# Experts' stage of a metaformer kernel: gating two blocks behind, pooled sums with the probabilities standing, choice on the logits, another order of the pools

## The chip, the cores and the metric

The kernel runs on one core of a Trainium2 chip. The metric is the device time of one execution in microseconds (us). Five engines take part, each with its own queue of instructions that it works off in order: PE (TensorE, matrix products and transposes; PEld are its loads of the standing operand), DVE (VectorE), ACT (ScalarE), POOL (GpSimd) and SP (SyncE), which here issues the DMAs.

## The reference, cut to what matters

The model is two metaformer layers on x of shape (4, 128, 64, 64): convolution with neighbourhood attention, a recurrence over the sequence, eight mamba layers, and a layer of experts that choose tokens. The change concerns the last of these. There are B = 4 sequences of S = 4096 tokens with D = 128 features, E = 64 experts with hidden size H = 512, and every expert takes the K = 8 tokens of a sequence with the highest probability.

```python
x = _ln_t(tokens)
logits = jnp.einsum('bsd,ed->bse', x, gate_w) + gate_b
probs = jax.nn.softmax(logits, axis=1)                 # over the tokens
vals, idx = jax.lax.top_k(probs.transpose(0, 2, 1), K)
...
pooled = jnp.einsum('bked,bke->bed', gathered, topv)    # sum of the 8 tokens by probability
h = gelu(einsum('ebd,edh->ebh', h, weight1))            # with a bias row
out = einsum('ebh,eho->ebo', h, weight2)                # with a bias row
...
outputs.at[arange(Bn)[:, None], flat_idx].add(weighted) # out by probability, back to the 8 tokens
```

The kernel does not gather. It makes a map of probabilities over all 4096 tokens that is zero except at an expert's eight tokens, and takes both sums as matrix products with that map.

## The kernel before

One program runs four stages one after the other: the conv layer, the recurrence, mamba and `experts`. The first three share a set of memory pools, which are released before the experts open theirs; a tile that is placed where an earlier one lay waits for the last use of the earlier one. The body stands under `tc.manual_schedule()`, so the order of the instructions on each engine's queue is the order in which the program writes them, and no scheduler moves any. In the experts' stage the order is therefore the one of the loop at L1386.

The four sequences are worked on as two pairs. A pair has 4096 tokens per sequence, in NBLK = 8 blocks of 512, so the loop runs n = 0 to 15 over blocks, and once more to finish. The feature dimension lies on the 128 partitions in the input, and the tiles are these:

- `fetch(n)` (L1233) loads block n of both sequences. It runs three blocks ahead.
- L1244 to L1259 load the gate's weights and the vector of biases, and make `both`: 128 columns that take the mean out of a token, and 64 columns of the gate's weights with the mean taken out.
- `tokens(n)` (L1269) does, for each of the two sequences, four products L1279 into `pa` (128 tokens by 192), copies the 128 token columns to a token slab (ACT, L1285) and the 64 gate columns to `raw` (ACT, L1286), squares the tokens (POOL, L1290) and sums the squares (DVE, L1291). Two small ACT instructions make 1/sigma of each token, `r` (L1293, L1294).
- `gating(n)` (L1296) multiplies `raw` by `r` (POOL, L1301), transposes it four times (PE, L1304), so that 2 x 64 (sequence, expert) rows lie on the partitions and tokens along the row, adds the bias into the logits `lg` (DVE, L1308) and takes the block's eight highest per row (DVE, L1309). In the loop it follows one block behind `tokens`: in iteration n, `tokens(n)` comes first and `gating(n - 1)` after it.
- `softmax(pr)` (L1313) takes the eight highest of the row, subtracts the highest in an exponential over all 4096 (ACT, L1321) that also sums, and makes the eight best probabilities. `scaled` (L1328) divides by the sum. `others` (L1333) writes `rest`, the row with its eight best replaced by zero.
- `pick(pr, i)` (L1340) subtracts `rest` from the row in block i (DVE, L1345), so that only the chosen ones remain, transposes the block back (PE, L1349), multiplies by `r` out of PSUM into `pk` (DVE, L1352), and adds the pooled sums up with eight products, one for each 128 tokens of each sequence: the 128 tokens x 128 features stand in the array and the 64 probabilities of a sequence move (PE, L1363, 16 records in the profile). `pooled` (L1368) copies the sums to `pz`.
- A ring of seven slabs of 2 MB holds the tokens (two slabs per pair) and the experts' weights. `give(s)` (L1377) issues the four DMAs of weight slab s. Slabs 0 to 2 are given during the loop, 3 and 4 take the place of pair 0's tokens, and the others follow when their slab is free.

Pair 0's softmax falls into iteration 9, its scaling and `others` into iteration 10, its picks two each into iterations 12 to 15. Pair 1's follow after the loop. Then come the experts' products L1429 (first weights) and L1464 (second weights, both with 32 standing columns in four column groups of one PSUM tile), and the output from L1485 on: the products of the map with the experts' outputs (L1498), the addition to x (L1505) and the stores.

## Time and profile before

| | us |
|---|---|
| median of 3 runs | 15860.6 (15850.09 to 15864.64) |
| the profiled execution's own time | 15855.17 |
| its span | 15853.2 |
| span of the experts' stage, from about 15510 on | some 343 |
| of it: picks of pair 1 | 15705.8 to 15748.2 |
| of it: weights, experts' products, output | 15748.2 to 15853.2 |

Times in the profile are microseconds from the start of the span. The groups of PE in the experts' stage are given as line, engine, operation, names (out<-in), shapes, count | busy us, mean ns of one | idle time of the engine before them, and what ended it:

```profile
L1279 PE MATMUL pa<-both,x 128*128 128x192 f32 x256 | 60.9, 408 | 1.1 <-DMA x<-x_d 1.1
L1363 PE MATMUL pp<-pk,slab 128*128 128x64 f32 x256 | 58.8, 424 | 12.5 <-DVE pk L1352 12.5
L1464 PE MATMUL po<-slab,hz 128*32 128x128 f32 x512 | 27.4, 342 | 12.3 <-DMA slab<-in_w_dram 11.4 <-DVE hz L1445 0.8
L1349 PE MATMUL pt<-ident,lg 128*128 128x128 f32 x64 | 17.1, 423 | 23.0 <-DVE lg L1345 23.0
L1304 PE MATMUL pg<-ident,raw 128*128 128x128 f32 x64 | 13.9, 356 | 47.1 <-POOL raw L1301 47.1
```

Records of PE overlap, so the mean of one is longer than the distance from one to the next. PE waited 47.1 us for the raw products of POOL, 23.0 us for DVE's subtractions and 12.5 us for DVE's `pk`.

### The profile page before, as it was taken

To read this page: it belongs to the slowest core of one execution; us is meant where nothing else is said; L and a number is where in the kernel's file an instruction comes from. 1 tells how busy PE (TensorE), PEld (TensorE's weight loads), DVE (VectorE), ACT (ScalarE), POOL (GpSimd) and SP (SyncE) were. 2 spreads that over 40 slices of the span, in tenths; PEclk is the share of its full clock that TensorE was granted. 3 is DMA by queue.
4 is the path that set the end of the run, shared out by engine and by line. 5 is a ranking of instruction groups with operands and counts; after the bars stand their busy time and mean duration, and the time that the engine had idled before them with its cause. 6 is when DMAs were issued, how large, how long until landed. Compare 5 with 4: busy or idle time off the path is not lost. (4 is left out here: it accounts for less than half of the span.)

```text
span 15853.2 us, 302528 instructions
## 1 busy us (share of the span) xinstructions
PE 14462.2 (91%) x120338; PEld 10877.7 (69%) x120338; DVE 13680.6 (86%) x14939; ACT 12003.3 (76%) x23543; POOL 13174.3 (83%) x9086
## 2 busy tenths in 40 slices
PE   7888779999999999999999999999999999989996
PEld 3444567777777777777777777777777777666665
DVE  8998049998999889998999899989998999899993
ACT  6887258887788778877888788878887788777771
POOL 4554049998999999998999899989998999899992
PEclk8999579999999999999999999999999999999997
DMA  0000012222222222222222222222222222222224
GB/s 21 22 25 19 15 57 103 98 97 104 97 103 103 95 102 98 99 107 95 103 99 98 100 98 103 103 99 101 99 98 102 99 103 100 96 99 94 101 102 153
DMA packets 423331, 1431.56 MB, mean 90 GB/s; under 512 B 204064, under 2 KB 204448, under 8 KB 290720
## 3 DMA queue, kind: packets, MB, share of 16 engines
q1 hardware_dynamic: 421920, 1412.21, 24.3%
q8 instruction: 951, 15.58, 0.4%
q14 instruction: 460, 3.77, 0.1%
HBM read 1353.34 MB, written 58.72 MB: 89 GB/s over the span
## 5 line engine op out<-in xcount | busy, mean ns | idle before, releaser
L1028 DVE TENSOR_TENSOR_SCAN hs<-dA,state,dBx 128x512 f32<-128x512 f32 x7168 | 8703.2, 1263 | 1048.9 <-PE dBx L995 1010.3
L1044 POOL TENSOR_TENSOR hs<-hs,Cb 128x2048 f32<-128x2048 f32 x2048 | 9294.1, 4538 | 165.8 <-POOL state L1041 1.3
L973 ACT ACTIVATE dA<-dt,A 128x512 f32<-128x512 f32 x7168 | 4734.5, 721 | 7.4 <-DVE hs L1028 1.2
L1048 PE MATMUL yT<-ident,hs 128*128 128x128 f32 x32768 | 4351.9, 277 | 7.5 <-POOL hs L1044 7.5
L1048 PEld LDWEIGHTS yT<-ident,hs 128*128 128x128 f32 x32768 | 3797.0, 144 | 771.3 <-issue 644.1
L995 PE MATMUL dBx<-diag,dtxT 64*128 64x128 f32 x57344 | 4191.7, 286 | 122.9 <-DVE hs L1028 110.5
L995 PEld LDWEIGHTS dBx<-diag,dtxT 64*128 64x128 f32 x57344 | 3518.0, 188 | 1087.3 <-issue 712.1
L672 ACT ACTIVATE z<-p 128x4 f32<-128x4 f32 x4096 | 710.2, 173 | 1855.2 <-PE p L669 1849.1
L669 PE MATMUL p<-z,vt 128*128 128x4 f32 x8192 | 1578.7, 263 | 205.2 <-ACT z L672 203.4
L669 PEld LDWEIGHTS p<-z,vt 128*128 128x128 f32 x8192 | 1350.5, 207 | 587.2 <-ACT z L672 303.2
L1016 POOL TENSOR_TENSOR hs<-Bb,dtx 128x512 f32<-128x512 f32 x1024 | 1274.0, 1277 | 0.3 <-PE yT L1048 0.3
L1028 DVE TENSOR_TENSOR_SCAN hs<-dAp,state,hs 128x512 f32<-128x512 f32 x1024 | 1228.5, 1262 | 0.0
L961 DVE TENSOR_TENSOR diag<-f,i 128x512 f32<-128x512 f32 x1792 | 1158.9, 671 | 8.3 <-PE f L949 8.3
L860 DVE SCALAR_TENSOR_TENSOR xc<-f,taps,xc 128x509 f32<-128x509 f32 (+2 forms) x1536 | 1131.3, 737 | 37.6 <-ACT tail L855 10.4
L1041 POOL COPY state<-hs 128x4 f32<-128x4 f32 x2048 | 386.7, 189 | 845.4 <-DVE hs L1028 844.9
L1126 ACT ACT_TABLE_LOAD x771 | 989.2, 1283 | 10.5
L278 DVE SCALAR_TENSOR_TENSOR acc<-qp,dww,acc 128x512 f32<-128x512 f32 x1184 | 888.7, 751 | 12.2
L973 ACT ACTIVATE dAp<-dt,A 128x512 f32<-128x512 f32 x1024 | 708.8, 692 | 212.7 <-DVE hs L1028 180.5
L875 PE MATMUL f<-u,given 128*128 128x512 f32 x1024 | 510.6, 621 | 331.1 <-ACT pos L1094 323.2
L849 ACT ACTIVATE xc<-f,taps 128x509 f32<-128x509 f32 x512 | 350.4, 684 | 478.1 <-PE f L846 476.0
L934 POOL TENSOR_TENSOR dtx<-dt,xc 128x512 f32<-128x512 f32 x512 | 650.5, 1271 | 12.4 <-ACT dt L928 12.4
L944 ACT COPY dtxT<-f 128x512 f32<-128x512 f32 x512 | 298.2, 582 | 445.2 <-PE f L941 445.2
(231 smaller groups left out, 16232.3 us busy)
## 6 DMA issues: line engine op xcount, KB each, us to landing
Cb<-c_d SPq DMA_DIRECT2D x1024, 1024.0 KB, 4.6
Bb<-c_d SPq DMA_DIRECT2D x256, 512.0 KB, 5.5
given<-in_m_given_dram SPq DMA_DIRECT2D x64, 640.0 KB, 5.8
slab<-in_w_dram SPq DMA_DIRECT2D x64, 512.0 KB, 10.2
x<-x_d SPq DMA_DIRECT2D x96, 256.0 KB, 3.9
x_d<-x SPq DMA_DIRECT2D x64, 256.0 KB, 2.0
c_d<-dbl SPq DMA_DIRECT2D x512, 32.0 KB, 1.6
xb<-in_x_dram SPq DMA_DIRECT2D x32, 256.0 KB, 3.0
```

What stands on the lines that cost most here:

```text
L278: nc.vector.scalar_tensor_tensor(rows(to), x, dww[:, t : t + 1], rows(o.acc), ALU.mult, ALU.add)
L669: nc.tensor.matmul(self.p[:, k, :], self.vt, self.before, start=False, stop=True, skip_group_check=True)
L672: nc.scalar.activation(self.z[:, k, :], self.p[:, k, :], AF.Tanh, scale=0.5)
L860: nc.vector.scalar_tensor_tensor(x, o.v[h][:, : TL - k], taps[:, o.l, h, DC - 1 - k : DC - k], x, ALU.mult, ALU.add)
L961: nc.vector.tensor_tensor(o.diag[:, sp], bt.unsqueeze(2).to_broadcast([P, NB, 64, 2]), i64.unsqueeze(1).unsqueeze(3).to_broadcast([P, NB, ...
L973: nc.scalar.activation(o.dA[j][:, k, :], o.dt[h], AF.Exp, scale=A[:, o.l, h, n : n + 1])
L995: nc.tensor.matmul(o.dBx[j][:, at : at + 64, :], o.dtxT[h][row, n, :], o.diag[row, sp, n], start=True, stop=True,)
L1016: nc.gpsimd.tensor_tensor(hs[:, k, :].rearrange("p (q n t) -> p q n t", n=NB, q=2), o.Bb[:, k, :].rearrange("p (q n t) -> p q n t", n=NB, ...
L1028: nc.vector.tensor_tensor_scan(hs[:, k, :], o.dA[j][:, k, :], hs[:, k, :] if sp == SP_B else o.dBx[j][:, :, k], state[:, o.l, o.b, h, s : ...
L1044: nc.gpsimd.tensor_tensor(hs, hs, o.Cb[f], ALU.mult)
L1048: nc.tensor.matmul(o.yT[:, n, :], x[:, n * P : (n + 1) * P], ops.ident, start=start and n == 0, stop=True, is_transpose=True, skip_group_c ...
L1126: return lambda o: nc.scalar.preload_act_table_set(name)
```

## The change

1. The pools of mamba are opened in another order. The sizes stay the same, but what lies where changes, and with it what of a later stage lies over it.
2. The gate's weights are loaded and prepared at the start of the kernel, in `gating_weights`, and kept in a pool that stays open. The small tiles it needs meanwhile are released again before the conv layer opens its pools.
3. `gating` follows two blocks behind `tokens` (LAG = 2), with a third buffer for `raw`; the loop runs to n = 17.
4. The choice is made on the logits: `others` replaces the eight highest logits by -1e30, and only then comes the exponential over 4096, in place. The picks take the exponential of `rest` block by block (a new ACT instruction in `pick`) and subtract. The division by the sum is no longer made over the row; `pooled` and the copy of `oh` multiply by the reciprocal instead.
5. `pick` is cut in two. `add_picked(pr, i)` follows one block behind. In it `pk` stands in the array, 32 columns at a time, in four column groups of one PSUM tile (2 sequences x 2 halves of the experts), and the 128 features of the tokens move: 16 products per block, of which the profile shows two records each. The sums come out transposed, and `pooled` transposes them back.
6. Pair 0's picks stand in iterations 11 to 14. Its pooled sums and the DMAs of weight slabs 3 and 4 stand in iteration 15.
7. The bias b1 is loaded as two tiles behind the picks of pair 1 in the program, in buffers that held blocks of x.

```diff
-        c = ctx.enter_context(tc.tile_pool(name="mc", bufs=1))
-        wp = ctx.enter_context(tc.tile_pool(name="mwp", bufs=2))
-        w1 = ctx.enter_context(tc.tile_pool(name="mw1", bufs=1))
-        w = ctx.enter_context(tc.tile_pool(name="mwk", bufs=2))
-        w3 = ctx.enter_context(tc.tile_pool(name="mwk3", bufs=3))
         dap = ctx.enter_context(tc.tile_pool(name="mda", bufs=4))
         hsp = ctx.enter_context(tc.tile_pool(name="mhs", bufs=4))
         cbp = ctx.enter_context(tc.tile_pool(name="mcb", bufs=4))
+        w3 = ctx.enter_context(tc.tile_pool(name="mwk3", bufs=3))
+        w = ctx.enter_context(tc.tile_pool(name="mwk", bufs=2))
+        c = ctx.enter_context(tc.tile_pool(name="mc", bufs=1))
+        wp = ctx.enter_context(tc.tile_pool(name="mwp", bufs=2))
         up = ctx.enter_context(tc.tile_pool(name="mu", bufs=5))
+        w1 = ctx.enter_context(tc.tile_pool(name="mw1", bufs=1))
...
-def experts(tc, ops, I, x3_d, out):
+def gating_weights(tc, const, ops, I):
+    nc = tc.nc
+    both = const.tile([P, P + E], F32, name="both")
+    gateb = const.tile([P, 1], F32, name="gateb")
+    nc.sync.dma_start(out=gateb, in_=I["vec"][:, V_GATEB : V_GATEB + 1])
+    nc.vector.tensor_tensor(both[:, 0:P], ops.ident, ops.avg, ALU.subtract)
+    with tc.tile_pool(name="gw", bufs=1) as w, tc.tile_pool(name="gp", bufs=1, space=PSUM) as ps:
+        gate = w.tile([P, E], F32, name="gate")
+        nc.sync.dma_start(out=gate, in_=I["gate"])
+        p = ps.tile([P, E], F32, name="p")
+        nc.tensor.matmul(p, both[:, 0:P], gate, start=True, stop=True)
+        nc.vector.tensor_copy(both[:, P:], p)
+    return both, gateb
+def experts(tc, ops, I, gating_w, x3_d, out):
...
         nc.scalar.preload_act_table_set(EXP_LN)
-        gate = c.tile([P, E], F32, name="gate")
-        nc.sync.dma_start(out=gate, in_=I["gate"])
-        vec = c.tile([P, V_N], F32, name="vec")
-        nc.sync.dma_start(out=vec, in_=I["vec"])
+        both, gateb = gating_w
         for n in range(3):
             fetch(n)
-        b1 = c.tile([P, NQ, HID], F32, name="b1")
-        nc.sync.dma_start(out=b1, in_=I["b1"])
         b2 = c.tile([P, E], F32, name="b2")
         nc.sync.dma_start(out=b2, in_=I["b2"])
-        both = c.tile([P, P + E], F32, name="both")
-        nc.vector.tensor_tensor(both[:, 0:P], ops.ident, ops.avg, ALU.subtract)
-        pq = psb.tile([P, BLK], F32, tag="pg", name="pq")
-        nc.tensor.matmul(pq[:, 0:E], both[:, 0:P], gate, start=True, stop=True)
-        nc.vector.tensor_copy(both[:, P:], pq[:, 0:E])
...
         def tokens(n):
-            raw = raws[n] = w.tile([P, 4, 2, E], F32, tag="raw", name="raw")
+            raw = raws[n] = w.tile([P, 4, 2, E], F32, tag="raw", name="raw", bufs=3)
...
                     pg[:, m * P : (m + 1) * P], raw[:, m].rearrange("p k e -> p (k e)"), ops.ident
                 )
             lg = lgs[pr][:, i * BLK : (i + 1) * BLK]
-            nc.vector.tensor_scalar(lg, pg, vec[:, V_GATEB : V_GATEB + 1], None, ALU.add)
+            nc.vector.tensor_scalar(lg, pg, gateb, None, ALU.add)
             nc.vector.max(out=tops[pr][:, i, :], in_=lg)
-        rests, bests, tots = {}, {}, {}
-        def softmax(pr):
+        rests, negs, tots = {}, {}, {}
+        def others(pr):
             lg = lgs[pr]
             top = w.tile([P, 8], F32, tag="top", name="top")
             nc.vector.max(out=top, in_=tops[pr].rearrange("p n t -> p (n t)"))
-            neg = w.tile([P, 1], F32, tag="neg", name="neg")
+            neg = negs[pr] = w.tile([P, 1], F32, tag="neg", name="neg")
             nc.vector.tensor_scalar(neg, top[:, 0:1], -1.0, None, ALU.mult)
+            rest = c.tile([P, NG * NHC, NJ * 36], F32, tag="rp", name="rest")
+            rests[pr] = rest.rearrange("p a b -> p (a b)")[:, 0:L]
+            nc.vector.match_replace(
+                out=rests[pr], in_to_replace=top, in_values=lg, imm_value=-1e30
+            )
             tot = tots[pr] = w.tile([P, 1], F32, tag="tot", name="tot")
             nc.scalar.activation(lg, lg, AF.Exp, bias=neg, accum_out=tot)
-            best = bests[pr] = w.tile([P, 8], F32, tag="best", name="best")
-            nc.scalar.activation(best, top, AF.Exp, bias=neg)
             nc.vector.reciprocal(tot, tot)
-            nc.vector.tensor_scalar(best, best, tot, None, ALU.mult)
-        def scaled(pr):
-            nc.vector.tensor_scalar(lgs[pr], lgs[pr], tots[pr], None, ALU.mult)
-        def others(pr):
-            rest = rests[pr] = c.tile([P, NG * NHC, NJ * 36], F32, tag="rp", name="rest")
-            nc.vector.match_replace(
-                out=rest.rearrange("p a b -> p (a b)")[:, 0:L],
-                in_to_replace=bests[pr], in_values=lgs[pr], imm_value=0.0,
-            )
-        pps = {}
+        pts, pps = {}, {}
         def pick(pr, i):
             here = slice(i * BLK, (i + 1) * BLK)
-            lg = lgs[pr][:, here]
-            rest = rests[pr].rearrange("p a b -> p (a b)")[:, here]
+            lg, rest = lgs[pr][:, here], rests[pr][:, here]
+            nc.scalar.activation(rest, rest, AF.Exp, bias=negs[pr])
             nc.vector.tensor_tensor(lg, lg, rest, ALU.subtract)
-            pt = psb.tile([P, BLK], F32, tag="pg", name="pt")
+            pts[i] = psb.tile([P, BLK], F32, tag="pg", name="pt")
             for m in range(4):
                 o = (4 * i + m) * P
-                nc.tensor.transpose(pt[:, m * P : (m + 1) * P], lgs[pr][:, o : o + P], ops.ident)
+                nc.tensor.transpose(
+                    pts[i][:, m * P : (m + 1) * P], lgs[pr][:, o : o + P], ops.ident
+                )
+        def add_picked(pr, i):
             pk = w.tile([P, 4, 2, E], F32, tag="pk", name="pk")
             r = rs[pr][:, 4 * i : 4 * i + 4, :]
             nc.vector.tensor_tensor(
                 pk,
-                pt.rearrange("p (m k e) -> p m k e", m=4, k=2),
+                pts.pop(i).rearrange("p (m k e) -> p m k e", m=4, k=2),
                 r.unsqueeze(3).to_broadcast([P, 4, 2, E]),
                 ALU.mult,
             )
             if i == 0:
-                pps[pr] = [psc.tile([P, E], F32, tag=f"pp{k}", name="pp") for k in range(2)]
+                pps[pr] = psc.tile([P, P], F32, tag="pp", name="pp")
             for m in range(4):
                 n = 4 * i + m
-                for k in range(2):
+                for g in range(4):
+                    k, half = divmod(g, 2)
                     nc.tensor.matmul(
-                        pps[pr][k], toks[pr][k][:, n, :], pk[:, m, k, :],
-                        start=n == 0, stop=n == NT - 1,
+                        pps[pr][32 * g : 32 * g + 32, :],
+                        pk[:, m, k, 32 * half : 32 * half + 32],
+                        toks[pr][k][:, n, :],
+                        start=n == 0, stop=n == NT - 1, skip_group_check=True,
                     )
         def pooled(pr):
+            ps = w.tile([P, P], F32, tag="os", name="ps")
+            nc.vector.tensor_scalar(ps, pps[pr], tots[pr], None, ALU.mult)
+            pt = psb.tile([P, BLK], F32, tag="pg", name="pt")
+            nc.tensor.transpose(pt[:, 0:P], ps, ops.ident)
             to = pz.rearrange("p m (j t) -> p m j t", t=36)
             for k in range(2):
                 nc.vector.tensor_copy(
-                    to[:, :, :, 2 * pr + k], pps[pr][k].rearrange("p (m j) -> p m j", j=NJ)
+                    to[:, :, :, 2 * pr + k],
+                    pt[:, k * E : (k + 1) * E].rearrange("p (m j) -> p m j", j=NJ),
                 )
         weights = {}
...
                 here = slice(n * (L // 4), (n + 1) * (L // 4))
                 nc.sync.dma_start(out=t[:, here], in_=I[which][s % 8][:, here])
+        LAG = 2
         give(0)
-        for n in range(2 * NBLK + 1):
+        for n in range(2 * NBLK + LAG):
             if n < 2 * NBLK:
                 tokens(n)
                 if n + 3 < 2 * NBLK:
                     fetch(n + 3)
-            if n == 4:
-                give(1)
-            if n == 7:
-                give(2)
-            if n > 0:
-                gating(n - 1)
-            if n == NBLK + 1:
-                softmax(0)
-            if n == NBLK + 2:
-                scaled(0)
+            if n in (4, 7):
+                give(1 + n // 7)
+            if n >= LAG:
+                gating(n - LAG)
+            m = n - NBLK - LAG
+            if m == -1:
                 others(0)
-            if n >= 2 * NBLK - 4:
-                for i in range(2):
-                    pick(0, 2 * (n - 2 * NBLK + 4) + i) if n < 2 * NBLK else None
-            if n == 2 * NBLK - 1:
+            elif 1 <= m <= 4:
+                for i in range(2 * m - 2, 2 * m):
+                    pick(0, i)
+                    if i > 0:
+                        add_picked(0, i - 1)
+            elif m == 5:
+                add_picked(0, NBLK - 1)
                 pooled(0)
-        give(3)
-        give(4)
-        softmax(1)
-        scaled(1)
+                give(3)
+                give(4)
         others(1)
-        for i in range(NBLK):
-            pick(1, i)
+        for i in range(NBLK + 1):
+            if i < NBLK:
+                pick(1, i)
+            if i > 0:
+                add_picked(1, i - 1)
         pooled(1)
         hz = c.tile([P, NG * NHC, NJ * 36], F32, tag="rp", name="hz")
         nc.gpsimd.memset(hz, 0.0)
         hids, x3b = {}, {}
+        b1 = [w.tile([P, HID], F32, tag=f"x3{q}", name="b1", bufs=3) for q in range(NQ)]
+        for q in range(NQ):
+            nc.sync.dma_start(out=b1[q], in_=I["b1"][q])
         for q in range(NQ):
             ph = psb.tile([P, HID], F32, tag="pg", name="ph")
             for s in range(4 * q, 4 * q + 4):
...
                             start=j == 0, stop=j == NJ - 1, skip_group_check=True,
                         )
             hid = hids[q] = w.tile([P, HID], F32, tag="sq", name="hid")
-            nc.vector.tensor_tensor(hid, ph, b1[:, q, :], ALU.add)
+            nc.vector.tensor_tensor(hid, ph, b1[q], ALU.add)
             nc.scalar.activation(hid, hid, AF.Gelu)
         ohT = c.tile([P, B, E], F32, name="ohT")
         for q in range(NQ):
...
                 pt[:, 0:P], ohT[:, 2 * pr : 2 * pr + 2, :].rearrange("p b e -> p (b e)"), ops.ident
             )
             oh = w.tile([P, P], F32, tag="oh", name="oh")
-            nc.vector.tensor_copy(oh, pt[:, 0:P])
+            nc.vector.tensor_scalar(oh, pt[:, 0:P], tots[pr], None, ALU.mult)
             for i in range(NBLK // 2):
                 pa = [psa.tile([P, 2, BLK], F32, tag="pa", name="pa") for k in range(2)]
                 for m in range(2):
...
     nc.scalar.preload_act_table_set(EXP_LN)
     ops = Ops(nc, const)
+    gating_w = gating_weights(tc, const, ops, I)
...
             conv_layer(tc, ops, I, x1_d, wx_d, stats)
             rec = Recurrence(c, tc, ops, I, stats, wx_d, x1_d, x2_d)
             mamba(tc, ops, I, rec, x2_d, x3_d)
-        experts(tc, ops, I, x3_d, out)
+        experts(tc, ops, I, gating_w, x3_d, out)
...
-    o["b1"] = np.repeat(w1[:, P].reshape(2, P // B, HID), B, axis=1).transpose(1, 0, 2)
+    o["b1"] = np.repeat(w1[:, P].reshape(2, P // B, HID), B, axis=1)
```

## The prediction

> **What bounds it.** The page first.
>
> ```profile
> span 15853.2 us, 302528 instructions
> PE   7888779999999999999999999999999999989996
> PEclk8999579999999999999999999999999999999997
> ```
>
> The experts run in the last of 40 slices of 396 us (from about 15510). Outside it the change touches the kernel's first microseconds and the opening order of the mamba pools, so every gain comes from some 340 us. The stage table cuts them (columns: busy us and records of PE, PEld, DVE, ACT, POOL; granted clock; DMA share; GB/s):
>
> ```profile
> 15618.00:15690.60 72.60, 50.41 (x220) 45.73 (x221) 18.78 (x30) 6.70 (x18) 10.27 (x10) 0.64 0.00 0
> 15690.60:15705.80 15.20, 1.24 (x6) 0.84 (x6) 10.20 (x12) 3.99 (x3) 0.00 (x0) 0.50 0.73 276
> 15705.80:15748.20 42.40, 36.10 (x160) 32.92 (x160) 9.74 (x16) 0.00 (x0) 3.94 (x1) 0.50 0.00 0
> 15748.20:15810.60 62.40, 48.33 (x651) 24.75 (x650) 4.21 (x14) 2.54 (x3) 0.00 (x0) 0.83 1.01 396
> 15810.60:15853.20 42.60, 31.06 (x67) 10.05 (x67) 20.17 (x20) 0.00 (x0) 0.00 (x0) 0.74 0.89 358
> ```
>
> Picks of pair 0 among the last tokens (PE), a softmax in which PE stands still, picks of pair 1 (PE), and a tail of 105 us that the weight and output DMAs fill. The tail begins when pair 1's last product frees its token slabs, so what comes before it moves the end one for one. The chain of waits shows one pick (start, us):
>
> ```profile
> 15705.83 1.10 PE pt L1349 x4
> 15706.93 0.02 issue
> 15706.95 0.70 DVE pk L1352
> 15707.65 0.04 issue
> 15707.70 3.67 PE pp L1363 x16
> 15711.37 0.87 PE pt L1349 x4
> ```
>
> Transposes, DVE, product, next transposes: strictly one after the other, 5.31 us each.
>
> **The new product's price.** No row of before has it. Nearest is L1464, which also has 128x32 standing operands, 128 moving columns and four column groups (timeline):
>
> ```profile
> 15785.64 1.93 PE L1464 MATMUL po<-slab,hz 128*32 128x128 f32 x32 [0.87 <-DMA slab<-in_w_dram]
> 15792.22 4.72 PE L1464 MATMUL po<-slab,hz 128*32 128x128 f32 x96 [0.38 <-DVE hz L1445]
> ```
>
> Its single records come in fours that start within 0.02 us, 0.213 us from four to four at half clock and 0.109 at full. A product becomes 32 records, 8 fours: 1.71 us cold, 0.87 warm, against 3.67. Bounds: 0.9 (warm), 3.7 (no gain), 6.8 (32 x 0.213, if the groups ran in turn). I take 1.8 cold (1.71 and 0.1 for the drain below), because L1464 has the operand shapes and the same accumulator shared by four groups. [...] The trace has such a place in the conv layer, L432 (110*32, last at 1626.62) to L440 (128*128, 1626.93): 0.31 us where the pitch was 0.11, so 0.2. [...] I take 0.1 a product (1.6 in all) and keep 5 more for the range.
>
> **The clock.** The second place. [...] But L1363 holds the array 0.213 us for 64 moving columns. The column-tiled products of L1429, from 15748.93 on, brought full clock after 2.5 us (0.72 as the mean of 15748.2 to 15754.0: 2.5 us of 5.8 at full). Around L1464, bursts of 32 every 2.56 us with pauses, the clock switched to and fro. The new picks (1.7 of product, 0.87 of transposes) are nearest to that row: I take half of pair 1's picks at full clock; all cold or all warm goes to the range. [...]
>
> **Part by part** (program order is issue order on each engine).
>
> *Gating weights at the start.* Two DMAs go ahead of conv's on SP, and conv's first load (L156, issued at 0.73) waits in the new layout for the gate's landing and the small matmul that reads it. Gate issued at 1.18 (where L158 stands), landing after 1.7 (as L1244's did), matmul 0.6: about 3.75. All later conv loads stand behind it and the first matmul waits for x (10.97, "5.90 <-DMA xb"). **+3.0** (2.5 to 4).
>
> *Experts' start.* L1244 stood at 15516.71 behind x_d's write, L1246 and the fetch at 15517.57 behind it. Now the fetch waits for none of these and follows the issue at 15514.64: about 15515.1. Landing (2.8) and first matmul (15520.41) follow: **-2.3**. The DVE/PE work of L1257 to L1259 was hidden in that landing.
>
> *Two blocks behind.* POOL's order remains square, square, raw product, so block n-2's raw product still stands behind block n's squares, and PE's transposes and next tokens behind it (raw L1301 1.04, then L1304 idles "2.79 <-POOL raw L1301"). The period (6.05/7.55) stays; only the beginning has a stall fewer: third transposes at 15536.65 for 15540.32, **-3.6**. The third raw buffer costs nothing.
>
> *Choice on logits, pair 0.* Out go the scaling (L1328, 2.33) and best; the match (4.41 plus 0.09) comes ahead of the big exponential (3.71 plus 0.19), which overwrites its input and must wait. From T, the iteration's transposes: T 0.66, lg 0.75, maximum 0.69, top, negation, hand-overs: 2.5; match to 7.05; exponential to 10.9. Behind it on ACT stands the next token copy; POOL and PE wait for it, 3.73 later the next T: 14.6 for 10.16, **+4.4**. Next iteration 6.8 for 8.93 (no DVE scaling before the variances): **-2.1**. Picks now sit in iterations 11 to 14: 11 has two sets of transposes and one product between T and the tokens (0.66 + 2.25 + 2 x 0.87 + 1.8 and 0.5 of hand-overs = 7.0, then 6.9 to the next T): 13.9 for 7.73, **+6.2**. The next three: T 0.66, wait for DVE 2.25, transposes 0.87, product 1.8, transposes 0.87, product 1.8, small change, together 8.7 to the tokens, then 6.9 as before: 15.6 for 20.88, 20.46, 20.46, **-15.1**. The new exponential of each rest block (about 0.7, as L1285's 0.59 and L973's 0.72) lies under lg and maximum on DVE. Sum **-6.6**.
>
> *From T of iteration 15 to pair 1's first pick.* Before: 15677.21 to 15705.83, 28.6, with two picks (some 13), then block 15's transposes, lg, maximum, and the softmax in series. After, walked engine by engine from T = 0: T ends 0.66; DVE lg and maximum to 2.1, the leftover pick's DVE step (0.70) to 2.8; its product 1.8 to 4.65; pooled's scaling and transpose to 5.6; the transposes of blocks 14 and 15, whose raw products POOL has long done, one behind the other to 7.4. DVE: the two pz copies to 6.2, lg and maximum of both blocks (2 x 1.45) to 9.4, top and negation to 9.85. Then in series match 4.5, exponential 3.9, the first block's exponential 0.7, subtraction 0.69, hand-overs 0.2: 19.8. Scaling (2.35), reciprocal and best are gone from this series. **-8.8**. DVE binds the middle of it, so a product of 3.7 here would cost 1.9 more.
>
> *Picks of pair 1.* The DVE step (0.70) now lies under the previous product. The blocks' exponentials (0.7 each, ACT has nothing else) run ahead of DVE. Cold: two transposes and a DVE step to fill (1.85), 8 products at 1.71, the six other transposes at 0.85, 0.3: 21, PE bound. Warm: DVE binds, 0.68 + 0.70 + 0.1 = 1.5 each, about 13.5. Half and half 17.3 for 42.3: **-25**.
>
> *Behind it.* Pooled's extra 0.86 (scaling 0.29, transpose 0.48, hand-over) lies before the first L1429 but under the weights' DMA (share 1.01), as does b1's 512 KB, issued behind the fifth slab while the DMAs are idle. oh's copy and scaling cost alike. Without that cover: 1 us. **0**.
>
> Sum: 3.0 - 2.3 - 3.6 - 6.6 - 8.8 - 25 = **-43.3**. The profiled execution took 15855.2 (span 15853.2), 5.4 below the median; it becomes 15812, the median 15860.6 - 43.3 = **15817**.
>
> **Rivals.**
> *A, the sum:* 0.75. With the picks all cold 15821, all warm 15813, give or take 6 for start, drain and the exposed chains: own range 15805 to 15828.
> *B, the swap brings nothing:* drains and 32 weight loads keep a product at 3.7. Each of 16 is 1.9 dearer than cold A (-39): -39 + 30 = -9, **15852**. For it: PEld is 32.9 of 42.4 in the third row, so weight loads matter here. Against: L1464 hides four loads in 0.213. Chance 0.10.
> *C, other side: the column groups run in turn,* 6.8 a product because all four share one accumulator tile: 16 x 5.0 = 80, -39 + 80 = +41, **15901**. It decides from 1.8 + 39/16 = 4.2 us a product up. Against: L1429 and L1464 share a tile in the same way. Chance 0.03.
> *D, the new mamba layout* changes scan or POOL durations: 5 ns on 8192 scans (1263) is 41 us either way. Against: scans reading dA from SBUF and dAp elsewhere take 1263 and 1262. If dearer, -43 + 41: **15858**. Chance 0.05, and 0.02 for a larger loss.
> *E, two blocks behind does decouple* the loop from POOL: some 2 us in 12 blocks, **15793**. The POOL order speaks against it. Chance 0.05.
>
> **Numbers.** 0.2% is 31.7 us, about what a measurement of this kernel tells from no change; the border is 15828.9. A and E lie below it: faster 0.80; same 0.15 (B, D); slower 0.05 (C, D worse). Left out of the range are C, half of B, two thirds of D, most of E and A's tails, together 0.2: 15797 to 15852; A's own stands above.
>
> **What would show it.** Right: 32 product records in 1.7 to 1.9 us (or 0.9) with no DVE wait between; pair 1's picks in 13 to 21; PE idle about 7 longer in iteration 9 and no L1328; the conv's x landing 3 later; scans still 1263 and 1277; the tail still 105. Wrong: products above 3; the token period below 6; a tail longer than 105, which would mean that DMA, not the picks, sets the end.

## The result, and the profile after

The median went from 15860.6 us (15850.09 to 15864.64) to 15805.72 us (15798.8 to 15814.28, 7 runs each): 54.9 us less, a ratio of 0.9967 with the 95% interval 0.9956 to 0.9979. The forecast was 15817. The profiled execution of the kernel after has a span of 15796.6 us, 56.6 less than before.

The stage table of the kernel after, cut at the same events as the one of before (picks of pair 0, softmax of pair 1, picks of pair 1, weights, output; the columns are us, busy us and records of PE, PEld, DVE, ACT, POOL, granted clock, DMA share, GB/s):

```profile
15605.60:15659.70 54.10, 33.90 (x336) 26.90 (x336) 20.59 (x31) 13.83 (x33) 12.35 (x13) 0.75 0.04 10
15659.70:15679.50 19.80, 4.83 (x46) 3.54 (x46) 11.38 (x17) 5.55 (x7) 1.98 (x2) 0.60 0.62 239
15679.50:15694.20 14.70, 14.63 (x288) 11.41 (x288) 9.46 (x15) 3.39 (x6) 3.76 (x1) 0.85 0.02 3
15694.20:15756.60 62.40, 45.16 (x654) 23.15 (x656) 5.37 (x18) 2.54 (x3) 0.17 (x1) 0.94 1.01 405
15756.60:15796.60 40.00, 28.81 (x65) 9.31 (x63) 19.26 (x17) 0.00 (x0) 0.00 (x0) 0.76 0.90 367
```

The third row is the one to look at. The picks of pair 1 take 14.7 us where they took 42.4, and the clock is 0.85 where it was 0.50. The timeline of PE shows how it comes (start, us, engine, line):

```profile
15679.47 1.94 PE L1345 MATMUL pt<-ident,lg 128*128 128x128 f32 x8 [12.28 <-DVE lg L1341]
15681.34 1.94 PE L1365 MATMUL pp<-slab,pk 128*32 128x128 f32 x32
15683.21 1.05 PE L1345 MATMUL pt<-ident,lg 128*128 128x128 f32 x4
15684.18 1.08 PE L1365 MATMUL pp<-slab,pk 128*32 128x128 f32 x32
15685.20 0.66 PE L1345 MATMUL pt<-ident,lg 128*128 128x128 f32 x4
15685.78 1.08 PE L1365 MATMUL pp<-slab,pk 128*32 128x128 f32 x32
```

No bracket stands behind the lines after the first: PE waits for nobody. The first product runs at half clock ("cold", 1.94), the second at full clock ("warm", 1.08), and from then on a pick costs 1.60 us, against 5.31 before.

The sum of the prediction can be held against the two profiled executions step by step. The events are those of the prediction; T is the block of gating transposes in an iteration.

| step | predicted | measured | from what |
|---|---|---|---|
| start of the kernel | +3.0 | +2.6 | conv's first product 10.94, then 13.50 |
| conv to the last scan, beyond that | 0 | -5.0 | last scan 15492.74, then 15490.27 |
| fetch at the experts' start | -2.3 | -2.4 | last scan to fetch 24.83, then 22.43 |
| two blocks behind | -3.6 | -1.1 | first token product to T of iteration 9: 68.22, then 67.15 |
| iterations 9 to 15 | -6.6 | -11.6 | T to T 88.61, then 77.05 |
| to pair 1's first pick | -8.8 | -8.9 | 28.59, then 19.71 |
| picks of pair 1 | -25 | -27.9 | 42.24, then 14.31, to the start of the last record |
| tail | 0 | -2.3 | 105.14, then 102.82 |
| sum | -43.3 | -56.6 | |

### The profile page after: what moved, and what is told of

Read it like the earlier page. It is cut to its first block, busy times and chain, and to the rows that moved or that the text cites. A ratio compares the mean times of both kernels' runs of the same rounds, so it can differ in the third digit from the quotient of the medians.

```text
span 15796.6 us, 303059 instructions
## 1 busy us (share of the span) xinstructions
PE 14414.7 (91%) x120596; PEld 10829.8 (69%) x120596; DVE 13673.8 (87%) x14937; ACT 12011.2 (76%) x23557; POOL 13179.6 (83%) x9086
## 3 DMA queue, kind: packets, MB, share of 16 engines
q1 hardware_dynamic: 422064, 1412.21, 24.8%
q14 instruction: 460, 3.77, 0.1%
## 5 line engine op out<-in xcount | busy, mean ns | idle before, releaser
L1028 DVE TENSOR_TENSOR_SCAN hs<-dA,state,dBx 128x512 f32<-128x512 f32 x7168 | 8699.2, 1262 | 1039.1 <-PE dBx L995 1003.3
L860 DVE SCALAR_TENSOR_TENSOR xc<-f,taps,xc 128x509 f32<-128x509 f32 (+2 forms) x1536 | 1129.9, 736 | 37.6 <-ACT tail L855 10.4
```

What stands on the lines that cost most here:

```text
L860: nc.vector.scalar_tensor_tensor(x, o.v[h][:, : TL - k], taps[:, o.l, h, DC - 1 - k : DC - k], x, ALU.mult, ALU.add)
L1028: nc.vector.tensor_tensor_scan(hs[:, k, :], o.dA[j][:, k, :], hs[:, k, :] if sp == SP_B else o.dBx[j][:, :, k], state[:, o.l, o.b, h, s : ...
```

## The experiments

Profiles of kernels that have the same code in a stage differ there by some us, so each verdict below is read first from the stage that the edit changes. For the whole experts' stage one number serves: the time from the first fetch to the end, 335.6 us before and 283.9 after. "Before beside it" is the median of the kernel before, run in turn with the kernel of the experiment; the ratio stands with its 95% interval.

**before_again**: the kernel before, unchanged, as a measure of that scatter.

> The kernel before, unchanged, for the scatter of the stages from one execution to the next. Experts' stage from fetch to end 335 to 337, picks of pair 1 42.2; the recurrence's start and mamba's length say how far two profiles of one kernel differ (5 to 10 if the differences seen so far are chance).

One time of 15847.01, and a span of 15845.0 for 15853.2. The picks of pair 1 took 42.25 again, exactly as before. But the recurrence began at 1659.24 for 1654.12, the last scan at 15487.23 for 15492.74, and the tail took 102.1 for 105.1. Fetch to end was 332.9 for 335.6. So the rows "conv to the last scan" (-5.0) and "tail" (-2.3) of the table lie within what one and the same kernel shows; the rows of the picks do not.

**old_product** and **wide_old**: what the swap is worth, and why. The first run is the kernel after with the old product:

```diff
-                for g in range(4):
-                    k, half = divmod(g, 2)
+                for k in range(2):
                     nc.tensor.matmul(
-                        pps[pr][32 * g : 32 * g + 32, :],
-                        pk[:, m, k, 32 * half : 32 * half + 32],
-                        toks[pr][k][:, n, :],
+                        pps[pr][k], toks[pr][k][:, n, :], pk[:, m, k, :],
```

> The kernel after, with the product in its old form (128 tokens x 128 features standing, 64 probabilities moving, 16 records) still one block behind; pooled has no transpose, and the pooled sums are not divided by the softmax's sum, so the output differs. Theory 1 (the swapped product is cheaper by itself and is what brings the clock to full): picks of pair 1 become PE bound at clock 0.5, 8 x (3.4 + 0.87), 35 to 37 us for 14.7; an iteration with two picks 17 to 17.5 for 13.8; in all about +35, 15840. Theory 2 (the gain is the pipelining, the product's price is about the same): picks of pair 1 at most 22, in all at most +12, 15805 to 15818.

The median was 15837.24 (before beside it 15856.38; ratio 0.9988, 0.9981 to 0.9995). The picks of pair 1 took 33.4 us and fetch to end 321.8: the swap is worth 37.9 of the 51.7 us that the experts' stage gained, as long as the rest of the change is there. Theory 1 holds, with the costs placed a little differently than expected: the picks took less (33.4 for 35 to 37), the iterations with two picks more (18.3 to 19.3 for 17 to 17.5). The second run changes one operand of that old product, so that 128 columns move where 64 did:

```diff
-                        pps[pr][k], toks[pr][k][:, n, :], pk[:, m, k, :],
+                        pps[pr][k], toks[pr][k][:, n, :], pk[:, m].rearrange("p k e -> p (k e)"),
```

> The run old_product with one edit: both sequences' 128 columns of pk move through each standing block of tokens instead of the 64 that belong to it (64 of the 128 sums are not used; the division by the sum is left out as before). Theory A (the clock follows the share of time in which columns move: 64 per 0.213 us kept it at half, 128 do not): full clock within some ten us, product 3.4 cold and 1.75 warm, picks of pair 1 in 19 to 23 us for 33.4, about 15820 for 15837. Theory B (only products in column groups bring full clock): product 3.4, clock 0.5, picks 33 to 34, 15837.

The median was 15809.83 (before beside it 15855.27; ratio 0.997, 0.9959 to 0.9982). The picks of pair 1 in the stage tables of the two runs, first old_product:

```profile
15701.50:15735.30 33.80, 33.80 (x160) 33.38 (x160) 9.74 (x16) 3.40 (x6) 3.94 (x1) 0.50 0.00 0
```

and wide_old:

```profile
15683.70:15704.30 20.60, 20.58 (x160) 20.20 (x160) 9.58 (x16) 3.44 (x6) 3.94 (x1) 0.87 0.01 2
```

Both have 160 records, and PE is busy all the time in both. The one that does twice the multiplications is done in 20.6 us instead of 33.8, since its clock is 0.87 instead of 0.50. In the timeline of old_product a product is the same in every pick, and in that of wide_old it halves after the first. One line of each:

```profile
15724.31 3.51 PE L1364 MATMUL pp<-pk,slab 128*128 128x64 f32 x16
```

```profile
15691.79 1.95 PE L1364 MATMUL pp<-pk,slab 128*128 128x128 f32 x16
```

So theory A holds in these two runs: with 64 columns moving through 128 standing ones PE was busy 33.80 of 33.80 us and the clock stayed at 0.50, with 128 it was 0.87. Fetch to end was 297.0. Of the 37.9 us of the swap, 24.8 (321.8 - 297.0) come with the clock alone, without any column groups; the other 13.1 are the product itself, 1.02 us from start to start at full clock instead of 1.79.

**swap_only**: the kernel before with the swapped product and nothing else; each pick still runs one after the other.

> The kernel before, with only the product swapped (and pooled's copy and transpose); every pick still runs one after the other. Theory 1: a pick of pair 1 is 0.87 + 1.05 + 1.8 = 3.75 at half clock, 30 for the eight (42.3 before), an iteration with two picks 3.6 shorter, in all about -26, 15835; if the swapped product brings full clock even with DVE's step between, picks of 2.6 to 2.9, 21 to 23 for the eight, 15825. Theory 2 (the pipelining is the gain): product 3 or more, at most -5, 15855 or more.

The median was 15828.38 (before beside it 15856.38; ratio 0.9982, 0.9974 to 0.9990), fetch to end 305.0, picks of pair 1 26.3 us. The expectation of 30 for a half clock and of 21 to 23 for a full one were both half right, as the stage table shows when it is cut where the products change:

```profile
15692.10:15712.80 20.70, 16.00 (x186) 11.16 (x187) 7.20 (x12) 0.00 (x0) 0.00 (x0) 0.51 0.01 2
15712.80:15718.70 5.90, 4.34 (x104) 3.27 (x104) 2.51 (x4) 0.00 (x0) 2.86 (x1) 1.00 0.01 3
```

Five picks passed at half clock, at 3.77 us each with 1.87 of product, and only then came the full clock. In the kernel after, with the DVE step out of the way, products fill 1.87 of 2.84 us at half clock and the full clock came at the second pick. When the clock changed can be read in the traces. Each of the 14 profiles has 218 to 244 records of the granted clock, and in each all of them begin on one grid of 3.413 us (off by at most 0.7% of a step). Cut along that grid, swap_only reads:

```profile
15702.23:15705.64 3.41, 2.63 (x36) 1.78 (x32) 1.13 (x2) 0.00 (x0) 0.00 (x0) 0.50 0.02 5
15705.64:15709.05 3.41, 2.63 (x40) 1.76 (x33) 0.93 (x3) 0.00 (x0) 0.00 (x0) 0.50 0.00 0
15709.05:15712.47 3.42, 2.95 (x36) 2.07 (x36) 0.94 (x2) 0.00 (x0) 0.00 (x0) 0.50 0.00 0
15712.47:15715.88 3.41, 2.31 (x60) 1.88 (x64) 2.15 (x4) 0.00 (x0) 0.04 (x1) 1.00 0.02 5
```

The kernel after and old_product each have a step that is busy throughout, and only the first of them is followed by the full clock (the next step of old_product is at 0.50 too):

```profile
15680.64:15684.05 3.41, 3.41 (x40) 2.47 (x38) 2.44 (x4) 2.25 (x4) 0.00 (x0) 0.50 0.02 5
15684.05:15687.46 3.41, 3.41 (x78) 2.54 (x80) 2.58 (x4) 0.00 (x0) 0.00 (x0) 1.00 0.02 5
15707.38:15710.79 3.41, 3.41 (x19) 3.41 (x18) 1.29 (x2) 0.00 (x0) 0.00 (x0) 0.50 0.00 0
```

A pick of swap_only is longer than a step, so its waits move against the grid by 0.36 us from pick to pick, until one step held little enough of them (PE busy 2.95 us for 2.63). The pipelined picks of the kernel after left no wait in the step from 15680.64 (PE busy 3.41 of 3.41 us), and the next step was at 1.00. The picks of pair 1 fell from 26.3 to 14.3 us between the two kernels, more than the eight waits for DVE of 0.78 us each: with the pipelining the full clock also came sooner, at the second pick instead of the sixth.

**lag1**: two blocks behind, taken back by one line.

```diff
-        LAG = 2
+        LAG = 1
```

> The kernel after with LAG = 1. Theory 1 (POOL's order holds the token loop, so two blocks behind is worth one stall at the beginning): the period of the plain iterations stays at 6.05 and 7.55, in all 0 to +4, 15804 to 15812. Theory 2 (two blocks behind frees the loop): plain iterations longer by 1 or more, +12 and above.

The median was 15802.09 (before beside it 15856.38; ratio 0.9965, 0.9952 to 0.9978), fetch to end 283.6 for 283.9. Between these two profiles, two blocks behind is worth nothing. **raw_first** shows why. It keeps LAG = 2 and issues POOL's product for block n-2 ahead of the squares of block n:

```diff
         for n in range(2 * NBLK + LAG):
+            if n >= LAG:
+                by_r(n - LAG)
             if n < 2 * NBLK:
                 tokens(n)
...
         def gating(n):
-            nc.gpsimd.tensor_tensor(raw, raw, r.unsqueeze(3).to_broadcast([P, 4, 2, E]), ALU.mult)
```

> The kernel after, with one move: POOL's product raw x r of block n-2 is issued ahead of the squares of block n instead of behind them. If POOL's order is what makes two blocks behind worthless (my theory): PE no longer waits 2.79 for POOL before the gating transposes, plain iterations fall from 6.05 and 7.55 to about 4.1 to 4.6, some 2.5 x 12 = 30 in all, about 15775. Rival (the loop is held by the way from tokens through ACT's copy, square and variance, whatever POOL's order): iterations stay within 0.5, at most -5, 15800.

The median was 15770.32 (before beside it 15860.28; ratio 0.9943, 0.9929 to 0.9958). A plain iteration of the kernel after, in the timeline:

```profile
15560.42 1.04 POOL L1306 TENSOR_TENSOR raw<-raw,r 128x512 f32<-128x512 f32 x1
15561.51 1.12 PE L1309 MATMUL pg<-ident,raw 128*128 128x128 f32 x4 [2.79 <-POOL raw L1306]
```

and one of raw_first:

```profile
15558.26 1.04 POOL L1305 TENSOR_TENSOR raw<-raw,r 128x512 f32<-128x512 f32 x1
15559.36 0.66 PE L1313 MATMUL pg<-ident,raw 128*128 128x128 f32 x4
```

In the first the transposes wait 2.79 us for POOL, as they did before the change. In the second nothing precedes them but PE's own work, and the iterations take 3.88 us each, where they took 6.05 and 7.55. Fetch to end fell from 283.9 to 251.9. The expectation was 4.1 to 4.6 an iteration, so the gain was somewhat larger than expected. No run moves the product with LAG = 1; how much of the 32.0 us needs the second block is not shown.

**probs**: the choice made on the probabilities again. Exponential over 4096 first, then the match, and no exponentials in the picks; the scaling stays gone.

```diff
+            nc.scalar.activation(lg, lg, AF.Exp, bias=neg, accum_out=tot)
+            nc.scalar.activation(best, top, AF.Exp, bias=neg)
             nc.vector.match_replace(
-                out=rests[pr], in_to_replace=top, in_values=lg, imm_value=-1e30
+                out=rests[pr], in_to_replace=best, in_values=lg, imm_value=0.0
             )
-            nc.scalar.activation(lg, lg, AF.Exp, bias=neg, accum_out=tot)
...
-            nc.scalar.activation(rest, rest, AF.Exp, bias=negs[pr])
```

> The kernel after, with the exponential over 4096 ahead of the match again and the match on the probabilities, no exponential in the picks (the scaling stays gone). Theory 1 (the choice on logits costs time by itself, because ACT waits for the match): iteration 9 shortens from 14.5 to about 10, iteration 10 grows by up to 2, the stretch to pair 1's first pick changes by -1 to +0.5; in all -2 to -5, about 15802. Theory 2 (the choice on logits is part of the gain): +3 or more.

The median was 15805.59 (before beside it 15856.38; ratio 0.9968, 0.9955 to 0.9981), no different from the kernel after, but the profile separates the two: iteration 9 takes 10.29 us for 14.50, iteration 10 takes 8.88 for 8.46, and the stretch to pair 1's first pick 19.3 for 19.7. Together that is -4.2, as theory 1 has it. These lines of the kernel after show the series:

```profile
15585.29 4.41 DVE L1327 MATCH_REPLACE8 rest<-top,lg 128x4096 f32<-128x4096 f32 x1
15589.74 3.71 ACT L1331 ACTIVATE lg<-lg,neg 128x4096 f32<-128x4096 f32 x1 [6.82 <-DVE rest L1327]
15597.18 1.11 PE L1309 MATMUL pg<-ident,raw 128*128 128x128 f32 x4 [11.24 <-POOL raw L1306]
```

The exponential waits for the match, the token copies stand behind the exponential on ACT, and PE stands 11.24 us. In probs it is 7.03 us:

```profile
15595.42 3.71 ACT L1326 ACTIVATE lg<-lg,neg 128x4096 f32<-128x4096 f32 x1 [2.42 <-DVE neg L1324]
15599.52 4.41 DVE L1332 MATCH_REPLACE8 rest<-best,lg 128x4096 f32<-128x4096 f32 x1
15603.05 1.12 PE L1309 MATMUL pg<-ident,raw 128*128 128x128 f32 x4 [7.03 <-POOL raw L1306]
```

What saved time at this place is that the division moved to the pooled sums, and that does not need the choice to be made on logits.

**start**: the gate's weights stay in the open pool and are loaded on ACT's queue.

```diff
-    nc.sync.dma_start(out=gateb, in_=I["vec"][:, V_GATEB : V_GATEB + 1])
+    nc.scalar.dma_start(out=gateb, in_=I["vec"][:, V_GATEB : V_GATEB + 1])
...
-        gate = w.tile([P, E], F32, name="gate")
-        nc.sync.dma_start(out=gate, in_=I["gate"])
+    gate = const.tile([P, E], F32, name="gate")
+    nc.scalar.dma_start(out=gate, in_=I["gate"])
```

> The kernel after, with the gate's weights at the start kept in the pool that stays open and loaded on ACT's queue, so that conv's first load waits for nothing. Conv's first product at 10.9 to 11.1 instead of 13.5. If that delay reaches the end as it is (my sum): -2.6, about 15802. If the later start of the recurrence (1661.7 to 1665.7 in the kernels with the new start, 1654.1 and 1656.6 in those with the old one) is a consequence of it: -7 to -10, the recurrence again at 1654 to 1657. If it is chance of the clock: the recurrence between 1654 and 1664.

The median was 15800.25 (before beside it 15860.28; ratio 0.9961, 0.9946 to 0.9976). In the kernel after, the timeline of the first microseconds shows the chain that the edit takes away:

```profile
1.18 0.42 SPq L1219 DMA_DIRECT2D gate<-in_gate_dram  x1
...
3.27 0.66 PE L1221 MATMUL p<-gate,both 128*128 128x64 f32 x2 [3.27 <-DMA gate<-in_gate_dram]
3.96 0.33 SPq L156 DMA_DIRECT2D vec<-in_vec_dram  x1
```

The load of `vec` is issued when the product that reads the gate is done, at 3.96; in the run start it is issued at 0.73, as before the change. Conv's first product came at 11.61 for 13.50 in this profile, and at 10.81 in that of best, which has the same edit. The recurrence began at 1659.9, within the range of all the others. A gain of 1.9 and 2.7 us at the start is seen; that it reaches the end is not shown, because times scatter more than that. The later start of the recurrence that the expectation asks about is scatter too: the kernel before has it at 1654.12 in one profile and at 1659.24 in the other.

**pools_only** and **after_old_pools**: mamba's pools in the new order in the kernel before, and in the old order in the kernel after.

> The kernel before, with mamba's pools opened in the new order and nothing else. If the layout has no price (my reading: scans 1262 or 1263 ns in all): first to last scan within 13281 to 13295, time 15850 to 15862. If the layout itself makes mamba cheaper: first to last scan at 13285 or below and the time at 15850 or below. The first fetch of the experts: still behind the writing of x_d by the gate's and the vector's loads, or 2 earlier if their place is free in the new layout.

> The kernel after, with mamba's pools opened in the old order. If the order only moves what the experts' first loads wait for: the fetch issues about 1.5 later behind the last scan (23.9 for 22.4), time 15803 to 15810. If the new order is what lengthens the time from conv's first product to the recurrence (1648 to 1656 in eight profiles with it, 1643 and 1646 in two without): back to 1643 to 1646 and 15795 to 15802, unless mamba gives it back (13281 to 13294 with it, 13292 and 13295 without).

The medians were 15850.31 (before beside it 15860.28; ratio 0.9994, 0.9985 to 1.0002) and 15795.51 (before beside it 15855.27; ratio 0.9961, 0.9947 to 0.9976). The scans had a mean of 1262 ns in pools_only and 1263 before. From the first to the last scan it took 13288.1 in pools_only and 13281.2 in after_old_pools, against 13295.2 and 13284.7 in the two profiles of the kernel before. No price and no gain of the order is seen. From conv's first product to the recurrence it took 1648.4 in after_old_pools, 1643.1 and 1648.7 in the two profiles of the kernel before: the order does not lengthen that either. My expectation that the fetch would come 1.5 later in after_old_pools was wrong: it stood 22.4 behind the last scan, as in the kernel after, and 23.3 in pools_only. The order takes 1.5 of the 2.4 us as long as the gate's loads are there; without them it takes nothing.

**best** and **blockwise**: what the runs together suggest. best joins raw_first, probs and start.

> The kernel after, with POOL's raw product first, the match on the probabilities again (exponential ahead of the match, no exponential in the picks), and conv's loads no longer behind the gate's weights. By the sum of the parts: -30 (loop), -5 (choice), -2.6 (start): about 15767. If the parts overlap, as iteration 9's gain may when its successors are shorter: 15770 to 15780. If the loop's gain does not come: 15797.

The median was 15760.88 (before beside it 15860.28; ratio 0.9938, 0.9921 to 0.9954), fetch to end 246.3. blockwise makes the exponential and the match of a block inside its pick:

```diff
+            nc.scalar.activation(
+                lg, lg, AF.Exp, bias=negs[pr], accum_out=parts[pr][:, i : i + 1]
+            )
+            nc.vector.match_replace(
+                out=rest, in_to_replace=bests[pr], in_values=lg, imm_value=0.0
+            )
```

> The run best, with the exponential and the match made block by block inside the picks (the sums of eight exponentials added up in pooled). If the 8.4 us in series ahead of the first pick are what is lost at both places: iteration 9 falls from 10.4 to about 4, iteration 10 from 14.2 to about 4, those with two picks grow by 1 to 2, the stretch to pair 1's first pick loses 7 and its picks gain 2 (DVE: 0.6 + 0.68 + 0.70 per block): about -18, 15743. If DVE becomes the bound in the picks (over 2.3 us a block): -10 or less.

The median was 15754.27 (before beside it 15855.27; ratio 0.9934, 0.9917 to 0.9950), fetch to end 240.0. The stretch to pair 1's first pick fell by 6.7, as expected. The two slow iterations fell only to 6.9 and 12.5 (from 10.4 and 14.2), and those with two picks grew by 0.4 to 1.8. PE waits there for DVE's subtraction, which now stands behind a match, 4.96 us where it waited 4.14 for it in best:

```profile
15590.12 1.08 PE L1352 MATMUL pt<-ident,lg 128*128 128x128 f32 x4 [4.96 <-DVE lg L1348]
```

So of the expected 18 us 6.3 came. Both versions are faster than the kernel after; between the two of them the intervals do not decide.

## Why the prediction was right, and where it was off

**The direction and most of the size** came from the picks of pair 1 and from the price of the new product. It was put at 1.8 us cold and 0.9 warm from the row of L1464; it measured 1.87 and 1.02 from start to start. The 0.1 taken a product for changes between column groups and whole transposes, and the 5 us kept beside it for the range, were the author's estimate: no run shows a drain as such. What the kernel after shows in its place is 0.16 us cold and 0.15 warm between the eight fours of a product (1.71 and 0.87) and the start of the next transposes. The row of the conv layer was misread: its last L432 record starts at 1626.73, not at 1626.62, so a change costs 0.09 us over the pitch there and not 0.2, and two of them 0.18, close to what was measured. Rivals B (no gain from the swap) and C (groups in turn, 6.8) fall with that row, D with pools_only. E falls as well: the periods of the plain iterations stayed at 6.06 and 7.54. What it forecast came only when raw_first changed POOL's order.

**The clock** was the right term with too small a size. The forecast took half of pair 1's picks as warm, a middle between its two bounds, since the clock went to and fro around L1464; seven of eight were. The full clock also stayed on for the token products behind pair 0's picks, 2.87 us for the 4.1 of before, which I had left as they were. One block of tokens in the kernel before, and one in the kernel after:

```profile
15649.86 4.10 PE L1279 MATMUL pa<-both,x 128*128 128x192 f32 x16
15640.33 2.87 PE L1284 MATMUL pa<-both,x 128*128 128x192 f32 x16
```

The second product of each of these iterations was partly warm as well (1.3 to 1.5 us for 1.8). T to T was 13.94, 13.80 and 13.74 instead of the 15.6 predicted, 5.3 us in all. The row "iterations 9 to 15" was off by 5.0, since iterations 10 and 11, +1.7 and -1.3, nearly cancel. That PE's busy time alone does not bring the full clock is seen in the picks of pair 1: busy 36.1 of 42.4 us at 0.50 in the kernel before, 33.80 of 33.80 us at 0.50 in old_product. What the prediction had beside it, 0.213 us a record for 64 moving columns, points at how much of the time columns move, and wide_old bears that out: 20.58 of 20.60 us busy with 128 moving, and 0.87.

How large the share of moving columns was in the steps that the full clock followed can only be estimated from the traces. I count 0.213 us at half clock for 128 moving columns (as in wide_old) and 0.32 for 192 (L1279 from record to record), four column groups side by side once, and 64 columns in proportion as 0.107, though their records lie 0.213 apart. By this estimate, up to the end of pair 1's picks the 14 profiles have 366 steps at half clock with work for PE. None of the 208 in which columns move for less than 0.74 of the step is followed by the full clock, though PE is busy at least 0.95 of the time in 38 of them. All 147 with 0.78 or more are; of the 11 between, 7. In swap_only the steps have 0.65 and the last one 0.74, in the kernel after 0.90, in old_product's picks of pair 1 at most 0.65.

**Two blocks behind** was predicted at -3.6 as a stall fewer at the beginning. That POOL's order keeps the period was right, and raw_first shows it. The step that failed is the credit for the missing stall. The stall did go: the transposes of iteration 2 came 15.7 us behind the first token product, for 19.9 before. But the next two periods ran longer at half clock than before (8.99 and 7.73 for 7.45 and 6.06 before) and gave 3.2 of it back, and with LAG = 1 the stage is as long. From profile to profile that loss went with where the clock's grid fell. In probs, which has the same code up to there, the two periods were 7.64 and 6.05 and the stretch to iteration 9 took 64.7 us, 3.5 less than before; its first mark of the grid lay 2.2 us behind the first token product. In the kernel after, old_product, wide_old, start and after_old_pools it lay 1.0 to 1.3 behind, and the first period took 8.94 to 9.01. Why the grid fell as it did is not known.

**The choice on logits** was predicted at +4.4 in iteration 9 and measured +4.3; PE's wait there grew by 4.35 us (11.24 for 6.89), not by the 7 that the list of signs names. Its successor was predicted at 6.8 and took 8.46: after 11 us of waiting the clock was at half (0.50 until 15602.1), and the token products took 4.8 us instead of 2.8. The stretch to pair 1's first pick, walked engine by engine, was 19.8 and measured 19.7.

**The start** (+3.0, measured +2.6) and **the fetch** (-2.3, measured -2.4) were right as single steps. The remaining 7.3 us of the difference (conv to the last scan, tail) belong to no step; before_again shows differences of that size between two profiles of the same kernel. That they fell on the side of the forecast is luck.

What stays open: 0.74 and 0.78 are an estimate from the f32 products and transposes of these 14 profiles, and no run varied the share of moving columns by itself in that range. What takes the clock away again was not worked out.

## What to carry to other kernels

Look at the moving columns per standing block of a product. In this kernel 64 columns held PE as long as 128 did (0.213 us a record at half clock in old_product and wide_old), and they left the clock at 0.50 although PE was busy 33.80 of 33.80 us. Swap the operands or fill the moving side, and then take out the waits between the products: the picks of pair 1 took 26.3 us with the swap and the waits still in (swap_only), 33.4 with the waits out and the old product (old_product), and 14.3 with both done (the kernel after). A larger distance between a producer and its consumer may bring nothing while the consumer's instruction stands behind the producer's next one on a queue that they share: here, with two blocks of distance, moving one instruction up on POOL's queue brought 32 us, and the distance without that move had brought nothing. And where a long instruction stands in a steady loop, look for the order in which the engine that feeds the loop is released first: with the exponential ahead of the match, PE stood 7.03 us instead of 11.24.

## What was not expected of the hardware

Doubling the moving columns of a product, 64 to 128 with the same 160 records, made a stage shorter by 13.2 us (33.8 to 20.6), through the clock alone (0.50 to 0.87). At half clock the 64 and the 128 columns cost the same, 0.213 us from one record to the next (old_product and wide_old, first pick of pair 1). The records of the granted clock begin on a grid of 3.413 us in each of the 14 profiles. A step at 0.50 in which PE was busy throughout was followed by another at 0.50 in old_product (from 15707.38) and by one at 1.00 in the kernel after (from 15680.64); by the estimate above, columns moved for at most 0.65 of the one and 0.90 of the other. The picks of swap_only, 3.77 us each beside that grid, ran cold for five rounds and turned warm in the sixth without any change in their work. And the clock carried over into what stood behind: the same 16 token products took 2.87 us behind the swapped and pipelined picks of the kernel after, 3.9 to 4.0 behind the swapped picks of swap_only, which wait, and 4.0 to 5.2 behind the old product.
